# A Mamba loop issued in the order of its text, with its head pieces one per step over 18 steps and its gather three steps behind the scan

## The chip, the cores and the metric

The kernel runs on one core of one Trainium2 chip. The metric is the device time of an execution in microseconds (us); smaller is better. "Before" means the kernel before the change, "after" the changed one.

The engines are TensorE (PE, with its weight loads PEld), VectorE (DVE), ScalarE (ACT), GpSimd (POOL) and SyncE. The trace lists the instructions of each (before has 38,998 on PE, 6,112 on DVE, 5,082 on ACT and 3,186 on POOL) and says for a wait which engine's work ended it.

## The reference, cut to what matters

Four layers follow each other: a non-local block, a convolution with one Mamba, two bidirectional Mambas (along the height, then along the width), and a dynamic filter. Only the Mamba loop of layers 1 and 2 changes.

```python
def _mamba(u, p):                       # u: N sequences, L positions, 64 channels
    xz = jnp.einsum('nld,ed->nle', u, p['in_proj_w'])
    x, z = jnp.split(xz, 2, axis=-1)                        # 128 channels each
    xc = conv1d_depthwise(x, 4 taps) ; x = silu(xc + conv_b)    # written short
    dt, Bm, Cm = jnp.split(jnp.einsum('nld,ed->nle', x, p['x_proj_w']), [4, 20], axis=-1)
    dt = jax.nn.softplus(jnp.einsum('nlr,dr->nld', dt, p['dt_proj_w']) + p['dt_proj_b'])
    A = -jnp.exp(p['A_log'])                                # 128 channels x 16 states
    def step(h, inp):
        dt_t, B_t, C_t, x_t = inp
        h = jnp.exp(dt_t[:, :, None] * A) * h + dt_t[:, :, None] * B_t[:, None, :] * x_t[:, :, None]
        return (h, jnp.einsum('nds,ns->nd', h, C_t))
    _, ys = jax.lax.scan(step, h0, ...)
    y = (jnp.swapaxes(ys, 0, 1) + x * p['Dp']) * jax.nn.silu(z)
    return jnp.einsum('nld,od->nlo', y, p['out_proj_w'])
```

## The kernel before

The work is cut into 120 units of 768 positions: 24 in layer 1, 96 in layer 2, where forward and reverse units alternate. A unit has 16 steps; one step handles 16 channels with their 16 states for 384 positions, as two blocks of 128 rows by 384 columns side by side. A step n consists of:

- `spread(n+1, n+2)`: four fp32 products on PE that lay u of the next step (u_s) and dt of the step after it (dt_s) out over the states, and on ACT the exponential da of dt_s;
- `scan(n)`: on DVE the multiply u_s x B and the scan h; on POOL the product hc = h x C;
- in every second step a `gather` on PE, which sums hc over the states into y_ssm.

```python
    def spread(self, now, later):
        ...                                   # 4 products: u_s, dt_s, u_s, dt_s
        if later is not None:
            da = self.work("da", bufs=4)
            with self.k.tc.issue_after(self.table.ins):
                self.nc.scalar.activation(da, u.pda[step][...], AF.Exp)
```

Beside the steps runs the **head** of the next unit (convolution, gate, softplus, B, C), in ten pieces. Each piece is one product (`mm`, or `conv` of four taps) into the same single PSUM bank, which ACT then empties. A `yield` hands back to the loop until the next step.

```python
    def head(self, u):                        # cut
        for j in range(2):
            p = self.convolved(u, ...)
            yield
            nc.scalar.activation(u.xc[:, halves[j]], p, AF.Identity, bias=w.conv_b)
        ...                                   # two gate pieces, Silu, load of a table
        for j in range(2):
            p = self.mm(w.step, u.xc[:, halves[j]])
            yield
            nc.scalar.activation(e[:, halves[j]], p, AF.Abs, bias=w.dt_b)
            nc.scalar.activation(u.dt[:, halves[j]], p, AF.Relu, bias=w.dt_b)
        ...
        for j in range(2):
            p = self.mm(w.bc[0], u.xc[:, halves[j]])
            yield
            nc.scalar.copy(u.B[:, halves[j]], p)
        ...                                   # the same for C; log, dt, u, memset on POOL
```

Each unit of layer 1 and each reverse unit of layer 2 also has a **tail**, the output product in two halves through the same bank. The loop of before starts the next unit's head in step 1 and then the tail:

```python
        for n, (u, s) in enumerate(steps):
            if s == 1:
                other = chain(after, before)          # head of next unit, tail of last
            self.spread(at(n + 1), at(n + 2))
            self.scan(u, s)
            next(other, None)                         # one piece
            if s % 2 == 0 and n >= 2:
                self.gather(*steps[n - 1])
```

A scheduler in the compiler then decides in which order each engine gets these instructions. The `yield` between a product and its emptying says nothing about the order in the built program of before.

Of the kernel before, what the change touches and what calls it, by code (L numbers as in the profile page):

```python
# [21 lines left out]
AF = mybir.ActivationFunctionType  # L22
ALU = mybir.AluOpType
# [5 lines left out]
L = H * W  # L29
# [462 lines left out]
class Mamba:  # L492
# [10 lines left out]


    STEPS = 16

    def __init__(self, k, tables, wk, ps_da, ps_u, ps_y, ps_m):
        self.k, self.nc, self.t = k, k.nc, tables
# [30 lines left out]
    def head(self, u):  # L539
        nc, w = self.nc, u.w  # L540
        halves = [slice(j * HALF, (j + 1) * HALF) for j in range(2)]
        rows = rows_of(u.b)


        raw = self.work("raw", 2 * CH)
        u.xc, u.gate = raw[:, :CH], raw[:, CH:]
        for j in range(2):
            p = self.convolved(u, u.c0 + j * HALF)
# [3 lines that stand above are left out]
            p = self.mm(w.gate_w[rows], self.k.xb[rows, u.c0 + j * HALF : u.c0 + (j + 1) * HALF])  # L552
            yield
            nc.scalar.copy(u.gate[:, halves[j]], p)

        self.k.tc.keep_in_program_order(nc.scalar.activation(raw, raw, AF.Silu))
        self.table = nc.scalar.preload_act_table_set("natural_log_exp_and_others")
        self.k.tc.keep_in_program_order(self.table)
        yield



        e, u.dt = self.work("e", bufs=1), self.work("dt")
# [5 lines that stand above are left out]
        nc.scalar.activation(e, e, AF.Exp, scale=-1.0)  # L569
        log = self.work("log", bufs=1)  # L570
        nc.scalar.activation(log, e, AF.Ln, bias=1.0)
        u.B, u.C = self.work("B"), self.work("C")
        for j in range(2):
            p = self.mm(w.bc[0], u.xc[:, halves[j]])
            yield
            nc.scalar.copy(u.B[:, halves[j]], p)
        kept = self.work("kept", bufs=1)
        nc.vector.tensor_scalar(kept, e, 1.0, 1.0, ALU.add, ALU.subtract)
        nc.gpsimd.tensor_sub(e, e, kept)  # L579
        nc.gpsimd.tensor_add(log, log, e)  # L580
        p = self.mm(w.bc[1], u.xc[:, halves[0]])
        yield
        nc.scalar.copy(u.C[:, halves[0]], p)
        nc.gpsimd.tensor_add(u.dt, u.dt, log)  # L584
        u.u = self.work("u")
        nc.gpsimd.tensor_mul(u.u, u.dt, u.xc)
        if not u.carry:

            first = W - 1 if u.rev else 0
            nc.gpsimd.memset(u.dt.rearrange("p (n t) -> p n t", t=W)[:, :, first : first + 1], 1e30)  # L590
        p = self.mm(w.bc[1], u.xc[:, halves[1]])
        yield
        nc.scalar.copy(u.C[:, halves[1]], p)

    def groups(self, step):

# [10 lines left out]
    def spread(self, now, later):  # L607
# [21 lines left out]
        if later is not None:  # L629
            u, step = later  # L630
            da = self.work("da", bufs=4)
            with self.k.tc.issue_after(self.table.ins):
                self.nc.scalar.activation(da, u.pda[step][:, NB - HALF : NB + HALF], AF.Exp)  # L633
            u.da[step] = da

    def scan(self, u, step):
# [13 lines left out]
        else:  # L650
            way = slice(None, None, -1) if u.rev else slice(None)
            nc.vector.tensor_tensor_scan(h[:, way], da[:, way], bx[:, way], 0.0, ALU.mult, ALU.add)  # L652
        hc = self.work("hc", bufs=5)
        nc.gpsimd.tensor_mul(two(hc), two(h), each(u.C))  # L654
        u.hc[step] = hc

# [22 lines left out]
    def run(self, units):  # L679
# [2 lines left out]
            u.pu, u.pda, u.da, u.hc = {}, {}, {}, {}  # L682
        steps = [(u, s) for u in units for s in range(self.STEPS)]
        at = lambda n: steps[n] if n < len(steps) else None
        for _ in self.head(units[0]):
            pass
        self.spread(None, at(0))
        self.spread(at(0), at(1))
        other = iter(())
        for n, (u, s) in enumerate(steps):  # L690
            i = n // self.STEPS
            if s == 1:
                before = units[i - 1].tail(units[i - 1]) if i else ()
                after = self.head(units[i + 1]) if i + 1 < len(units) else ()
                other = chain(after, before)
            if s == self.STEPS - 2:
                for _ in other:
                    pass
            self.spread(at(n + 1), at(n + 2))
            self.scan(u, s)  # L700
            next(other, None)
            if s % 2 == 0 and n >= 2:
                self.gather(*steps[n - 1])
        self.gather(*steps[-1])
        for _ in units[-1].tail(units[-1]):
            pass


# [11 lines left out]
def layer1(k):  # L720
# [41 lines left out]
    with ExitStack() as pools:  # L762
# [10 lines left out]
        def tail(u):  # L773
            rows = rows_of(u.b)
            for j in range(2):
# [3 lines left out]
                out = k.xa[rows, u.c0 + j * HALF : u.c0 + (j + 1) * HALF]  # L779
                nc.vector.tensor_add(out, out, p[rows, :HALF])  # L780

        m.run(
            [
                SimpleNamespace(w=w, b=b, c0=c0, rev=False, carry=carries[b], tail=tail)
                for c0 in range(0, L, CH)
                for b in range(B)
            ]
        )


def layer2(k):
# [5 lines left out]
def bi_mamba(k, which, along_h, lin_w, lin_b):  # L797
# [27 lines left out]
    with ExitStack() as pools:  # L825
# [46 lines left out]
        for c0 in range(0, L, CH):  # L872
            for b in range(B):
                f = SimpleNamespace(w=w[0], b=b, c0=c0, rev=False, carry=None, tail=no_tail)
                r = SimpleNamespace(w=w[1], b=b, c0=c0, rev=True, carry=None, tail=tail, forward=f)
                units += [f, r]
        m.run(units)


def layer3(k, out):  # L880
# [134 lines left out]
```

## Time and profile before

| | before |
|---|---|
| time | 10,242.94 us, median of 3 (10,217.05 to 10,250.11) |
| unit, layer 1 / layer 2 along H / along W | 59.3 / 56.6 / 55.8 us |
| mean granted clock in the loop, same parts | 0.78 / 0.84 / 0.84 |
| outside the loop | about 3,410 us |

The unit times are the distances between the Silu of successive units.

Then two groups of PE, with busy time, mean ns of one, and the idle time before them with what ended most of it:

```profile
L622 PE MATMUL u_s<-u,spread 32*128 32x384 f32 x7680 | 2221.5, 629 | 429.3 <-DVE h L652 325.5
...
L513 PE MATMUL mm<-raw,bc 128*128 128x384 f32 x960 | 519.2, 627 | 27.7 <-ACT dt L568 23.0
```

The second says that the head's products almost never wait. From the view of waits, the weight loads that go ahead of such a product (us in total, times, longest). They wait more often than the products: at 7030.12 PEld has been idle for 0.55 us before such a load, ended by ACT's copy of B, and PE not at all before the product:

```profile
PEld mm L513 <- ACT B L576: 123.1, 213, 1.7
```

And a window over 47 units of layer 2 (window, length, then busy us of PE, PEld, DVE, ACT, POOL, then the clock):

```profile
4528.20:7187.00 2658.80, 2263.99 (x10676) 751.71 (x10676) 2083.68 (x1667) 1132.36 (x1544) 1771.98 (x1068) 0.84 0.00 1
```

DVE is busy for 2,084 of 2,659 us. The rest is what a better order could win.

### The profile page before, as it was taken

What the parts mean: (1) busy time and instruction counts of PE and PEld (TensorE: products, weight loads), DVE (VectorE), ACT (ScalarE), POOL (GpSimd) and SP (SyncE); (2) the same over time, 40 slices, a digit from 0 to 9 for tenths busy, and PEclk for the clock granted to TensorE, in tenths of its full rate; (3) what the DMA queues carried; (4) which work ended last, traced back from release to release, by engine and by line L of the source; (5) the groups of instructions that cost most, each with busy time, mean ns of one, the idle gap of its engine ahead of it and who ended that gap; (6) DMA issues with size and microseconds to landing.
All of it is one profiled execution on the core that took longest, in us unless ns stands there. A gap on an engine that the chain in (4) does not pass through costs nothing.

```text
span 10211.9 us, 100390 instructions
## 1 busy us (share of the span) xinstructions
PE 8743.6 (86%) x38998; PEld 2948.9 (29%) x38998; DVE 7503.5 (73%) x6112; ACT 4291.8 (42%) x5082; POOL 4701.9 (46%) x3186
## 2 busy tenths in 40 slices
PE   9999999999868888868888888888688888888884
PEld 3333333333222222222222222222222222222221
DVE  4666646666658777767787777777778777787778
ACT  3444434444334334434444444444344444444442
POOL 0000000000036666636666666666367666676663
PEclk9999989999977777768888888888688888898887
DMA  0000000000000000000000000000000000000000
GB/s 24 1 1 1 1 1 1 1 1 1 1 0 1 1 1 1 1 0 1 1 1 1 1 1 1 1 1 1 0 1 1 1 1 1 1 1 1 1 1 19
DMA packets 2220, 17.25 MB, mean 2 GB/s; under 512 B 196, under 2 KB 324, under 8 KB 1096
## 3 DMA queue, kind: packets, MB, share of 16 engines
q1 hardware_dynamic: 1440, 9.44, 0.2%
q8 instruction: 307, 5.03, 0.2%
q14 instruction: 177, 1.45, 0.0%
q10 hardware_dynamic: 296, 1.33, 0.0%
HBM read 6.05 MB, written 4.72 MB: 1 GB/s over the span
## 4 chain that ended last, share of the span: by engine, by line
PE 27%; DVE 24%; POOL 15%; issue 5%; ACT 2%; DVEq 0%; POOLq 0%; ACTq 0%
DVE h L652 13%; PE u_s L622 7%; POOL hc L654 7%; DVE u_s L642 7%; PE y_ssm L665 6%; PE conv L536 4%; PE mm L513 4%; POOL e L579 2%; POOL log L580 2%; POOL dt L584 2%; PE dt_s L622 1%; PE conv L530 1%; DVE h L648 1%; POOL yg L677 1%; PE lin L863 1%
## 5 line engine op out<-in xcount | busy, mean ns | idle before, releaser
L654 POOL TENSOR_TENSOR hc<-h,C 128x768 f32<-128x768 f32 x1920 | 3484.0, 1819 | 1746.0 <-DVE h L652 1551.5
L652 DVE TENSOR_TENSOR_SCAN h<-da,u_s 128x768 f32<-128x768 f32 x1536 | 2693.8, 1754 | 199.5 <-DVE u_s L642 4.8
L633 ACT ACTIVATE da<-dt_s 128x768 f32<-128x768 f32 x1920 | 1554.2, 809 | 2936.6 <-PE dt_s L622 2914.2
L642 DVE TENSOR_TENSOR u_s<-u_s,B 128x768 f32<-128x768 f32 x1920 | 1825.6, 951 | 1146.0 <-PE dt_s L622 1059.0
L622 PE MATMUL u_s<-u,spread 32*128 32x384 f32 x7680 | 2221.5, 629 | 429.3 <-DVE h L652 325.5
L622 PE MATMUL dt_s<-dt,decay 32*128 32x384 f32 x7680 | 2119.3, 630 | 8.7 <-ACT da L633 3.5
L267 DVE TENSOR_TENSOR acc_e<-acc_e,e 128x1536 f32<-128x1536 f32 x792 | 1390.0, 1755 | 763.4 <-ACT e L211 724.7
L665 PE MATMUL y_ssm<-hc,gather 128*32 128x384 f32 x7680 | 1433.9, 598 | 457.9 <-POOL hc L654 456.6
L211 ACT ACTIVATE e<-f_exp 128x1536 f32<-128x1536 f32 x864 | 1207.0, 1449 | 1218.4 <-PE f_exp L201 1218.4
L622 PEld LDWEIGHTS u_s<-u,spread 32*128 32x128 f32 x7680 | 775.5, 217 | 1871.8 <-DVE h L652 805.9
L240 POOL TENSOR_TENSOR xa<-xa,t_att 64x512 f32<-64x512 f32 x36 | 45.3, 1259 | 2725.1 <-ACT t_att L238 2725.1
L218 PE MATMUL y_att<-e,xb 128*64 128x512 f32 x5184 | 1242.5, 601 | 0.0
L201 PE MATMUL f_exp<-theta,phi 64*128 64x512 f32 x5184 | 1235.7, 608 | 0.6 <-ACT e L211 0.6
L536 PE MATMUL conv<-xb,taps 64*128 64x384 f32 (+3 forms) x1536 | 694.2, 604 | 118.2 <-ACT raw L550 117.5
L648 DVE TENSOR_TENSOR_SCAN h<-da,state,u_s 128x384 f32<-128x384 f32 x768 | 737.4, 1000 | 48.4 <-DVE u_s L642 1.0
L622 PEld LDWEIGHTS dt_s<-dt,decay 32*128 32x128 f32 x7680 | 692.4, 217 | 186.7 <-ACT da L633 126.7
L201 PEld LDWEIGHTS f_exp<-theta,phi 64*128 64x128 f32 x5184 | 468.8, 187 | 756.7 <-issue 463.4
L665 PEld LDWEIGHTS y_ssm<-hc,gather 128*32 128x32 f32 x7680 | 232.0, 116 | 1429.7 <-POOL hc L654 854.4
L218 PEld LDWEIGHTS y_att<-e,xb 128*64 128x64 f32 x5184 | 341.3, 136 | 830.7 <-issue 830.1
L513 PE MATMUL mm<-raw,bc 128*128 128x384 f32 x960 | 519.2, 627 | 27.7 <-ACT dt L568 23.0
L550 ACT ACTIVATE raw<-conv,cols 128x384 f32<-128x384 f32 x240 | 139.6, 582 | 909.6 <-PE conv L536 415.1
L536 PEld LDWEIGHTS conv<-xb,taps 64*128 64x128 f32 x1536 | 332.7, 227 | 457.1 <-ACT raw L550 180.4
(147 smaller groups left out, 6005.7 us busy)
## 6 DMA issues: line engine op xcount, KB each, us to landing
xa<-in_x SPq DMA_DIRECT2D x6, 768.0 KB, 10.1
out<-xb SPq DMA_DIRECT2D x4, 1152.0 KB, 4.4
mats<-in_mats ACTq DMA_DIRECT2D x1, 1218.0 KB, 7.8
cols<-in_cols ACTq DMA_DIRECT2D x1, 71.5 KB, 9.5
dtw<-in_dtw ACTq DMA_DIRECT2D x1, 10.0 KB
```

Of the source, the lines that this page charges most:

```text
L201: nc.tensor.matmul(fs[j // 3][:, bass.ts(j % 3, NB)], lhsT=phi[at, bass.ts(m // 2, P)], rhs=theta[at, bass.ts(i, NB)], start=True, stop=True,)
L211: nc.scalar.activation(e, f, AF.Exp)
L218: nc.tensor.matmul(y[rows_of(m % 2)], lhsT=g[:, m, :], rhs=es[j // 3][:, bass.ts(j % 3, NB)], start=m < 2, stop=m >= KEYS - 2,)
L267: nc.vector.tensor_add(acc, acc, e)
L513: self.nc.tensor.matmul(p[:, :HALF], lhsT=lhsT, rhs=rhs, start=True, stop=True)
L536: self.nc.tensor.matmul(p3[:, :, o], lhsT=lhsT, rhs=x3[:, :, i], **flags)
L622: self.nc.tensor.matmul(self.side((u.pu if what == 0 else u.pda)[step], j), lhsT=(self.t.spread if what == 0 else u.w.decay)[rows, q], rhs ...
L633: self.nc.scalar.activation(da, u.pda[step][:, NB - HALF : NB + HALF], AF.Exp)
L642: nc.vector.tensor_mul(two(bx), two(bx), each(u.B))
L652: nc.vector.tensor_tensor_scan(h[:, way], da[:, way], bx[:, way], 0.0, ALU.mult, ALU.add)
L654: nc.gpsimd.tensor_mul(two(hc), two(h), each(u.C))
L665: nc.tensor.matmul(u.py[32 * r : 32 * r + 32, :HALF], lhsT=self.t.gather[:, q], rhs=u.hc[s][:, j * HALF : (j + 1) * HALF], start=q == 0, s ...
```

## The change

Its intent is to take the order out of the scheduler's hands and spread the work evenly, so that DVE, the engine with the most unavoidable work (45.4 us in a unit of layer 2 against PE's 34 at full clock, by the prediction's sums), never waits: head pieces one per step over 18 steps instead of bunched, POOL's chain of four pieces pulled apart, gathers late enough never to wait for POOL.

```diff
+    LEAD = 18
...
-        raw = self.work("raw", 2 * CH)
+        raw = self.work("raw", 2 * CH, bufs=3)
...
-        for j in range(2):
-            p = self.mm(w.bc[0], u.xc[:, halves[j]])
-            yield
-            nc.scalar.copy(u.B[:, halves[j]], p)
-        kept = ...; nc.gpsimd.tensor_sub(e, e, kept)      (these three put short)
+        for t, lhsT in ((u.B, w.bc[0]), (u.C, w.bc[1])):
+            for j in range(2):
+                p = self.mm(lhsT, u.xc[:, halves[j]])
+                yield
+                nc.scalar.copy(t[:, halves[j]], p)
+                if lhsT is w.bc[0] and j == 1:
+                    kept = ...; nc.gpsimd.tensor_sub(e, e, kept)
+
         nc.gpsimd.tensor_add(log, log, e)
         yield
+        yield
         nc.gpsimd.tensor_add(u.dt, u.dt, log)
+        yield
+        yield
         u.u = self.work("u")
         nc.gpsimd.tensor_mul(u.u, u.dt, u.xc)
...
-            with self.k.tc.issue_after(self.table.ins):        (and two more such hints)
-                self.nc.scalar.activation(da, ...)
+            self.nc.scalar.activation(da, ...)
...
-        hc = self.work("hc", bufs=5)
+        hc = self.work("hc", bufs=7)
...
+            i, ahead = (n + self.LEAD) // self.STEPS, (n + 2) // self.STEPS
+            if i not in heads and 0 < i < len(units):
+                heads[i] = self.head(units[i])
...
+            if s == self.STEPS // 2 + 1 and n > s:
+                before = units[n // self.STEPS - 1]
+                tail = before.tail(before)
             self.spread(at(n + 1), at(n + 2))
             self.scan(u, s)
-            next(other, None)
-            if s % 2 == 0 and n >= 2:
-                self.gather(*steps[n - 1])
+            for one in (*heads.values(), tail):
+                next(one, None)
+            if s % 2 == 0 and n >= 4:
+                self.gather(*steps[n - 3])
...
-        m.run(units)
+        with tc.manual_schedule():
+            m.run(units)
```

With `manual_schedule` the text is the program. The head's `yield` between product and emptying now does mean that the copy is issued one step later, after the next `spread` and its da.

More of the change, by code (lines that the diff above doesn't have):

```diff
@@ L554, in head @@
             nc.scalar.copy(u.gate[:, halves[j]], p)
-        self.k.tc.keep_in_program_order(nc.scalar.activation(raw, raw, AF.Silu))
-        self.table = nc.scalar.preload_act_table_set("natural_log_exp_and_others")
-        self.k.tc.keep_in_program_order(self.table)
+        nc.scalar.activation(raw, raw, AF.Silu)
+        nc.scalar.preload_act_table_set("natural_log_exp_and_others")
         yield
@@ L572, in head @@
         u.B, u.C = self.work("B"), self.work("C")
-        for j in range(2):
-            p = self.mm(w.bc[0], u.xc[:, halves[j]])
-            yield
-            nc.scalar.copy(u.B[:, halves[j]], p)
-        kept = self.work("kept", bufs=1)
-        nc.vector.tensor_scalar(kept, e, 1.0, 1.0, ALU.add, ALU.subtract)
-        nc.gpsimd.tensor_sub(e, e, kept)
+        for t, lhsT in ((u.B, w.bc[0]), (u.C, w.bc[1])):
[4 more added lines that the diff above has]
+                if lhsT is w.bc[0] and j == 1:
+                    kept = self.work("kept", bufs=1)
+                    nc.vector.tensor_scalar(kept, e, 1.0, 1.0, ALU.add, ALU.subtract)
+                    nc.gpsimd.tensor_sub(e, e, kept)
         nc.gpsimd.tensor_add(log, log, e)
-        p = self.mm(w.bc[1], u.xc[:, halves[0]])
         yield
-        nc.scalar.copy(u.C[:, halves[0]], p)
+        yield
         nc.gpsimd.tensor_add(u.dt, u.dt, log)
+        yield
+        yield
         u.u = self.work("u")
@@ L590, in head @@
             nc.gpsimd.memset(u.dt.rearrange("p (n t) -> p n t", t=W)[:, :, first : first + 1], 1e30)
-        p = self.mm(w.bc[1], u.xc[:, halves[1]])
-        yield
-        nc.scalar.copy(u.C[:, halves[1]], p)
     def groups(self, step):
@@ L631, in spread @@
             da = self.work("da", bufs=4)
-            with self.k.tc.issue_after(self.table.ins):
-                self.nc.scalar.activation(da, u.pda[step][:, NB - HALF : NB + HALF], AF.Exp)
+            self.nc.scalar.activation(da, u.pda[step][:, NB - HALF : NB + HALF], AF.Exp)
             u.da[step] = da
@@ L684, in run @@
         at = lambda n: steps[n] if n < len(steps) else None
+        heads = {}
         for _ in self.head(units[0]):
@@ L688, in run @@
         self.spread(at(0), at(1))
-        other = iter(())
+        tail = iter(())
         for n, (u, s) in enumerate(steps):
-            i = n // self.STEPS
-            if s == 1:
-                before = units[i - 1].tail(units[i - 1]) if i else ()
-                after = self.head(units[i + 1]) if i + 1 < len(units) else ()
-                other = chain(after, before)
-            if s == self.STEPS - 2:
-                for _ in other:
-                    pass
+            i, ahead = (n + self.LEAD) // self.STEPS, (n + 2) // self.STEPS
+            if i not in heads and 0 < i < len(units):
+                heads[i] = self.head(units[i])
+            if ahead in heads and (n + 2) % self.STEPS == 0:
+                for _ in heads.pop(ahead):
+                    pass
+            if s == self.STEPS // 2 + 1 and n > s:
+                before = units[n // self.STEPS - 1]
+                tail = before.tail(before)
             self.spread(at(n + 1), at(n + 2))
             self.scan(u, s)
-            next(other, None)
-            if s % 2 == 0 and n >= 2:
-                self.gather(*steps[n - 1])
+            for one in (*heads.values(), tail):
+                next(one, None)
+            if s % 2 == 0 and n >= 4:
+                self.gather(*steps[n - 3])
+        self.gather(*steps[-3])
         self.gather(*steps[-1])
-        for _ in units[-1].tail(units[-1]):
+        for _ in chain(tail, units[-1].tail(units[-1])):
             pass
@@ L780, in tail @@
                 nc.vector.tensor_add(out, out, p[rows, :HALF])
-        m.run(
-            [
-                SimpleNamespace(w=w, b=b, c0=c0, rev=False, carry=carries[b], tail=tail)
-                for c0 in range(0, L, CH)
-                for b in range(B)
-            ]
-        )
+        units = [
+            SimpleNamespace(w=w, b=b, c0=c0, rev=False, carry=carries[b], tail=tail)
+            for c0 in range(0, L, CH)
+            for b in range(B)
+        ]
+        with tc.manual_schedule():
+            m.run(units)
 def layer2(k):
@@ L876, in bi_mamba @@
                 units += [f, r]
-        m.run(units)
+        with tc.manual_schedule():
+            m.run(units)
 def layer3(k, out):
```

## The prediction

> **What bounds the kernel now.** I read the page first: busy time per engine, the clock row, the groups. Then the timeline of two units of work, then the clock in short windows.
>
> ```profile
> PE 8743.6 (86%) x38998; PEld 2948.9 (29%) x38998; DVE 7503.5 (73%) x6112; ACT 4291.8 (42%) x5082; POOL 4701.9 (46%) x3186
> ...
> L652 DVE TENSOR_TENSOR_SCAN h<-da,u_s 128x768 f32<-128x768 f32 x1536 | 2693.8, 1754 | 199.5 <-DVE u_s L642 4.8
> ...
> L642 DVE TENSOR_TENSOR u_s<-u_s,B 128x768 f32<-128x768 f32 x1920 | 1825.6, 951 | 1146.0 <-PE dt_s L622 1059.0
> ```
>
> The Mamba loop is 120 units (24 in layer 1, 96 in layer 2) of 16 steps. A step is u_s and dt_s on PE, da on ACT, a multiply and a scan on DVE, hc on POOL; every second step a gather on PE. Windows over whole units gave 1363.5 us for 23 units of layer 1 (59.3 each) and 2662.0 and 2626.2 us for 47 units of layer 2 each (56.3 on average): 24 x 59.3 + 96 x 56.3 = 6830 us. The other 3410 us are not touched.
>
> Multiplies in an undisturbed row start 2.745 us apart (7051.72, 7054.46). 16 steps plus one kept (0.45) and two yv (0.5 each) make 45.4 us, so some 11 us of a layer-2 unit are waits of DVE. The third quoted line says for what: 1059 us for PE, before the multiply. PE itself has room: at full clock 16 spreads of 0.86, 8 gathers of 0.78, two conv halves of 2.7, eight mm of 0.85 and about 2 of tail are 34 us of 56. It waits and is then slow:
>
> ```profile
> 7030.50:7033.90 3.40, 3.07 (x16) 0.75 (x14) 3.27 (x4) 2.31 (x4) 3.30 (x2) 1.00 0.02 5
> 7033.90:7037.30 3.40, 0.00 (x0) 0.00 (x0) 3.26 (x3) 0.00 (x0) 3.34 (x2) 1.00 0.00 0
> 7037.50:7040.70 3.20, 3.12 (x13) 0.80 (x13) 0.00 (x0) 0.00 (x0) 3.14 (x5) 0.50 0.00 0
> ...
> 7057.90:7061.10 3.20, 1.46 (x11) 0.55 (x10) 3.07 (x3) 0.87 (x2) 2.69 (x3) 1.00 0.00 0
> 7061.30:7064.60 3.30, 3.30 (x7) 1.79 (x6) 1.87 (x2) 0.21 (x1) 1.99 (x2) 0.50 0.03 7
> ```
>
> Columns: window, length, then busy us of PE, weight loads, DVE, ACT, POOL, then the granted clock. A stretch with PE at 0.00 of 3.40, or 1.46 of 3.20, is followed by one at clock 0.50, in which the same spread takes 1.65 instead of 0.92. Over the loop the clock is 0.78 (layer 1) and 0.84 (layer 2).
>
> What before does right shows in its timeline:
>
> ```profile
> 7030.12 0.91 PE L513 MATMUL mm<-raw,bc 128*128 128x384 f32 x2
> ...
> 7030.27 0.81 ACT L633 ACTIVATE da<-dt_s 128x768 f32<-128x768 f32 x1 [0.69 <-PE dt_s L622]
> 7031.07 0.48 ACT L576 COPY B<-mm 128x384 f32<-128x384 f32 x1
> ...
> 7032.19 0.91 PE L513 MATMUL mm<-raw,bc 128*128 128x384 f32 x2
> 7032.36 0.81 ACT L633 ACTIVATE da<-dt_s 128x768 f32<-128x768 f32 x1 [0.81 <-PE dt_s L622]
> ...
> 7033.04 0.84 PE L665 MATMUL y_ssm<-hc,gather 128*32 128x384 f32 x4
> 7033.14 0.48 ACT L583 COPY C<-mm 128x384 f32<-128x384 f32 x1
> ```
>
> A head piece (mm) goes to PE straight after a spread, and ACT empties its bank (the only one for such pieces) in the same step, after that step's da. When the next piece comes, the bank is long free.
>
> [...]
>
> **The change part by part.** No operation is added or removed; order and buffers change.
>
> The program order of the changed kernel, as built, has in each step PE: spread, then mm(k), then (even steps) gather; ACT: da, then the emptying of mm(k-1). So mm(k) waits for a copy that stands behind a da that waits for the spread just ahead of mm(k). That is a ring, PE to ACT to PE, once per step, for the eleven steps after a unit's head begins (step 15 of one unit to step 9 of the next). Its length at full clock, from the timeline: spread start to dt_s end 0.92; to da 0.10; da to copy 0.80 (7030.27 to 7031.07); copy 0.48; to mm 0.05; mm to the next PE work 0.85 (7032.19 to 7033.04): 3.20 us, and 3.98 with a gather, against DVE's 2.745. Steps with Abs and Relu (about 1.05) in place of a copy are 0.55 longer.
>
> Other in-order waits, layer 2:
> - Step 14: dt_s of the next unit stands between the halves of u_s(15) and waits for the memset behind u<-dt,raw on POOL, issued in step 13. hc(13) starts 2.97 after its step; +1.8 +1.8 +0.2: PE resumes about 4.15 after step 14 begins and u_s(15) is there at 5.1, not 2.75.
> - conv halves of 2.7 each ride on steps 14 and 15, gate pieces on 0 and 1.
> - Step 2: Silu and two table loads hold ACT 4.05 us; DVE just bridges it. yv there waits for a late gather.
> - Tail (every second unit in layer 2, every unit in layer 1): its second half waits for DVE to empty the bank in step 10, and step 10's gather, for which DVE's yv waits, is behind it.
>
> Carried through by hand, step after step (a start is the later of DVE's 2.745 and the ring's arrival), starts of the multiplies in us after step 14:
>
> | step | 15 | 0 | 1 | 2 | 3 | 4 | 5 | 6 | 7 | 8 | 9 | 10 | 11 | next 14 |
> |---|---|---|---|---|---|---|---|---|---|---|---|---|---|---|
> | start | 5.1 | 9.5 | 14.65 | 18.8 | 23.35 | 26.1 | 29.25 | 33.8 | 37.5 | 41.5 | 44.7 | 48.7 | 51.95 | 60.2 |
>
> So 60.2 us at full clock: 45.4 of DVE and 14.8 of waits. A unit with a tail: lin's three matmuls of about 0.75 twice on the ring, DVE waiting from 51.5 to 56.3 for yv: 65.6. Mean 62.9. Layer 1 the same way with 2.92 per step (from its timeline), no memset wait, longer DVE, a short tail in each unit: 59.7.
>
> What it gains: before's run of four POOL pieces that held hc (DVE waited 3.43 us at 7040.72) is spread over steps 7 to 13, where POOL (1.8 + 1.8 in such a step, 1.8 in the next) catches up; gathers three steps back never wait for hc. Both are inside the figures above, since no such wait appears in them.
>
> Sum at full clock: layer 2 96 x (62.9 - 56.3) = +630; layer 1 +10. That compares my full clock with before's mixed one. A ring leaves PE holes of 1.5 us in most steps and over 3 in steps 14 and 3, so windows of half-busy PE are common: I take the clock as about 0.80, near layer 1's 0.78. About 28 of 63 us are PE work that stands on the ring (spread and mm or conv of eleven steps, six gathers). In a stretch at half clock such work takes twice as long; with 40% of the time at half clock, some 0.4 x 28 x 0.6 = 7 us per unit are added (0.6 because part of the holes fills first, a guess). 120 x 7 = 840, of which I count 500 to 840. Total 10243 + 640 + 500 to 840 = 11,380 to 11,720.
>
> **The rivals.**
> - *DVE becomes the bound.* This is what the change means to reach: 45.4 us and about 1.2 of half the tails, 46.6 per layer-2 unit and about 51 in layer 1, which saves 96 x 9.7 + 24 x 8 = 1120, giving 9,120. For it: the steps 4 to 10 of before that run at 2.745. Against it: the ring is longer than 2.745 in eleven of sixteen steps, whatever the clock.
> - *The ring at a steady clock.* Evenly spread PE work keeps the clock full: 10,880. For it: the ring's steps with bc pieces are as dense as steps of before that kept it. Against: the 4 us hole in step 14, just before conv.
> - *Half gained, half lost.* If a wait I put on the ring is missing in truth (a bank freed earlier, a shorter start), each of eleven steps loses only 0.3 and the time stays about 10,250.
> - *Low clock for good.* At half clock the ring is 1.65 + 0.10 + 0.80 + 0.48 + 0.05 + 1.6 = 4.7, or 6.1 with a gather, 5.4 on average; eleven of these and the rest make over 75 us per unit: 12,400.
>
> **Range and chances.** The order on each engine is known, and every term of the ring is read from the trace, so the sign is fairly sure; the clock is not. I take 11,400 us, 10,700 to 12,000. Faster by over 2%: 0.10, for a ring that isn't there; within 2%: 0.07; slower by over 2%: 0.83.
>
> **What would show it.** Right: in the changed profile DVE's idle time before the multiply grows from 1146 us to over 2000, released by PE; mm waits for ACT's copies (B, C, raw) in hundreds of cases; ACT's copy follows a da that ended just before; dt_s waits for POOL about 4 us once per layer-2 unit; units of layer 2 take 62 to 70 us, tail units about 5 more than others. Wrong: multiplies 2.75 apart while bc pieces run, or a mean clock over 0.92, which would make me wrong on the ring or on the clock; POOL as the releaser of the scan would mean that the lag I took as caught up isn't.

## More of the kernel before

The prediction shows the busy times and the stretches at half clock. What will be needed for the comparison beside that is, first, the clock row of the page: the span in 40 slices, each digit the granted clock in tenths.

```profile
PEclk9999989999977777768888888888688888898887
```

The first eleven slices lie ahead of the loop; then it comes, at 7 in layer 1 and mostly 8 in layer 2.

## The result, and the profile after

Ratios here are the mean time of one kernel's fast runs over that of the other's of the same rounds, so they are not quite the ratio of the medians that are quoted.

| | before | after |
|---|---|---|
| time, median of 4 | 10,229.99 us (10,191.12 to 10,250.11) | 12,625.9 us (12,614.82 to 12,628.78) |
| ratio | 1 | 1.2346 (1.2305 to 1.2386) |
| unit, layer 1 / 2 along H / along W | 59.3 / 56.6 / 55.8 | 73.8 / 77.8 / 77.4 |
| loop clock, same parts | 0.78 / 0.84 / 0.84 | 0.66 / 0.67 / 0.67 |

Slower, as predicted, but outside the predicted range of 10,700 to 12,000. The units account for all of it: 24 x 14.5 + 48 x 21.2 + 48 x 21.6 = 2,400 us, against 2,396 between the medians. From the page of after, the busy times and the clock row:

```profile
PE 9649.2 (77%) x38998; PEld 3175.5 (25%) x38998; DVE 7572.6 (60%) x6112; ACT 4218.6 (33%) x5082; POOL 4702.0 (37%) x3186
...
PEclk9999899996666665666666666666766666666666
```

The number of PE instructions is the same, and PE is busy for 906 us longer with them, while its share of the span falls. After the first slices the clock row is at 6 almost throughout. The groups:

```profile
L642 DVE TENSOR_TENSOR u_s<-u_s,B 128x768 f32<-128x768 f32 x1920 | 1840.8, 959 | 2957.7 <-PE dt_s L623 2953.8
L623 PE MATMUL u_s<-u,spread 32*128 32x384 f32 x7680 | 2845.7, 751 | 609.9 <-DVE h L652 476.3
...
L514 PE MATMUL mm<-raw,bc 128*128 128x384 f32 x960 | 536.6, 647 | 695.9 <-ACT B L577 312.7
```

DVE's idle time before the multiply grew from 1,146 to 2,958 us, all of it released by PE. The same spread product takes 751 ns instead of 629. The head's B and C products, which waited 28 us before, wait 696 us. The view of waits says how often:

```profile
DVE u_s L642 <- PE dt_s L623: 2953.8, 1081, 12.4
...
PEld mm L514 <- ACT dt L568: 692.0, 240, 3.0
PEld mm L514 <- ACT B L577: 557.0, 240, 2.5
...
PEld dt_s L623 <- POOL dt L594: 334.8, 96, 5.5
```

240 is every one of two pieces in 120 units: the products wait for ACT each time. The last line is the wait for the memset, once per unit of layer 2. (PEld is the weight load of a product. At 10376.89 both start together, PEld after 1.94 us of idle time and PE after 1.33, each ended by ACT's copy.)

A window over the same 47 units:

```profile
4875.80:8532.00 3656.20, 2655.51 (x10644) 847.94 (x10644) 2098.97 (x1662) 1102.38 (x1541) 1767.84 (x1066) 0.67 0.00 0
```

DVE, ACT and POOL do the same work as before to within 3%; only PE's work takes longer and everything else waits. The clock records of the trace hold two values only, 1.00 and 0.50 (414 stretches of each in after); in this window 67% of the time is at 0.50 and 33% at 1.00, which gives the 0.67.

The ring is easiest to see in the timeline where the clock is full (start, duration, engine, and in brackets the idle time before and what ended it):

```profile
10374.64 0.58 PE L623 MATMUL u_s<-u,spread 32*128 32x384 f32 x1
...
10375.66 0.81 ACT L633 ACTIVATE da<-dt_s 128x768 f32<-128x768 f32 x1 [1.92 <-PE dt_s L623]
10376.36 0.47 ACT L577 COPY C<-mm 128x384 f32<-128x384 f32 x1
...
10376.89 0.91 PE L514 MATMUL mm<-raw,bc 128*128 128x384 f32 x2 [1.33 <-ACT C L577]
10377.73 0.85 PE L665 MATMUL y_ssm<-hc,gather 128*32 128x384 f32 x8
...
10378.52 0.58 PE L623 MATMUL u_s<-u,spread 32*128 32x384 f32 x1
```

Spread on PE, then da on ACT, then the copy of the piece of the step before, then PE may put the next piece into the bank, then the gather, then the next spread: 10378.52 - 10374.64 = 3.88 us, while DVE needs 2.745. Two steps earlier the same ring runs at half clock:

```profile
10366.60 0.81 ACT L633 ACTIVATE da<-dt_s 128x768 f32<-128x768 f32 x1 [0.70 <-PE dt_s L623]
10367.30 0.47 ACT L577 COPY B<-mm 128x384 f32<-128x384 f32 x1
...
10367.83 1.65 PE L514 MATMUL mm<-raw,bc 128*128 128x384 f32 x2 [1.31 <-ACT B L577]
...
10369.41 1.51 PE L665 MATMUL y_ssm<-hc,gather 128*32 128x384 f32 x8
...
10372.52 0.97 DVE L642 TENSOR_TENSOR u_s<-u_s,B 128x768 f32<-128x768 f32 x1 [2.66 <-PE dt_s L623]
```

The product takes 1.65 instead of 0.91 and the gather 1.51 instead of 0.85, ACT's part is unchanged, and DVE has been idle for 2.66 us when the spread is there. The hole in step 14 looks like this:

```profile
10396.72 1.64 PE L623 MATMUL u_s<-u,spread 32*128 32x384 f32 x2 [1.81 <-DVE h L652]
...
10398.57 1.80 POOL L590 TENSOR_TENSOR u<-dt,raw 128x768 f32<-128x768 f32 x1
...
10400.43 0.11 POOL L594 MEMSET dt<- 128x8 f32 x1
...
10400.59 1.00 PE L623 MATMUL dt_s<-dt,decay 32*128 32x384 f32 x1 [2.23 <-POOL dt L594]
```

PE has put half of u_s(15) out, then stands until POOL has finished u<-dt,raw and the memset behind it, though only dt_s needs them; the other half of u_s(15) is behind dt_s. Last, the clock itself around this hole, in stretches of 3.3 to 3.4 us with the same columns as above:

```profile
10389.40:10392.80 3.40, 1.71 (x16) 0.47 (x16) 3.21 (x4) 0.81 (x1) 2.27 (x2) 1.00 0.00 0
10392.80:10396.10 3.30, 0.93 (x8) 0.31 (x8) 3.17 (x3) 0.81 (x1) 3.08 (x2) 1.00 0.00 0
10396.30:10399.60 3.30, 1.64 (x2) 0.49 (x2) 2.98 (x3) 0.00 (x0) 2.79 (x2) 0.50 0.00 0
10399.70:10403.00 3.30, 2.41 (x8) 1.02 (x9) 0.71 (x1) 0.67 (x1) 2.56 (x3) 0.50 0.00 0
10403.10:10406.40 3.30, 3.30 (x7) 1.80 (x6) 1.91 (x2) 0.04 (x1) 1.11 (x1) 0.50 0.00 0
10406.50:10409.80 3.30, 3.30 (x18) 0.72 (x16) 0.00 (x0) 0.00 (x0) 0.59 (x1) 0.50 0.00 0
```

PE is busy for 0.93 of 3.30 us in the second stretch, and the next is at 0.50. But in the last two PE is busy all the time and the clock is still 0.50; in this place it stays there for 47.8 us (10396.18 to 10443.97), with PE busy for 37.88 of them. That is what I had not reckoned with.

Step by step, the distance from one multiply to the next, mean over the units of layer 2 along W. The second column is the difference of successive starts in the prediction's table:

| step | predicted, full clock | after | in after, median at half clock |
|---|---|---|---|
| 14 | 5.1 | 5.71 | 5.7 |
| 15 | 4.4 | 8.25 | 8.4 |
| 0 | 5.15 | 8.24 | 8.4 |
| 1 | 4.15 | 6.10 | 6.1 |
| 2 | 4.55 | 6.34 | 6.6 |
| 3 | 2.75 | 2.76 | 2.76 |
| 4 | 3.15 | 3.06 | 3.1 |
| 5 | 4.55 | 6.35 | 6.4 |
| 6 | 3.7 | 4.11 | |
| 7 | 4.0 | 5.90 | 5.8 |
| 8 | 3.2 | 3.10 | |
| 9 | 4.0 | 3.88 (full clock in all) | |

The prediction is right to about 0.1 us in steps 8 and 9, which run at full clock, and in 3 and 4, which are at half clock in about half of the units and lose nothing by it. Steps 15, 0, 1, 2, 5 and 7, mostly at half clock, are 1.8 to 3.9 us longer than predicted, step 14 by 0.6. Left out are steps 11 to 13, close to what DVE needs (3.1, 2.75 and 2.74 us), and step 10, where a unit with a tail takes 8.05 us and another 3.27.

### The profile page after: what moved, and what is told of

Same layout as the page of the kernel before. It is cut to its first block, busy times and chain, and to the rows that moved or that the text cites. A ratio compares the mean times of both kernels' runs of the same rounds, so it can differ in the third digit from the quotient of the medians.

```text
span 12613.0 us, 100405 instructions
## 1 busy us (share of the span) xinstructions
PE 9649.2 (77%) x38998; PEld 3175.5 (25%) x38998; DVE 7572.6 (60%) x6112; ACT 4218.6 (33%) x5082; POOL 4702.0 (37%) x3186
## 3 DMA queue, kind: packets, MB, share of 16 engines
q10 hardware_dynamic: 296, 1.33, 0.0%
## 4 chain that ended last, share of the span: by engine, by line
PE 36%; DVE 9%; ACT 7%; issue 6%; POOL 4%; DVEq 0%; POOLq 0%; ACTq 0%
PE u_s L623 9%; PE conv L537 8%; PE mm L514 8%; PE y_ssm L665 5%; DVE h L652 4%; PE dt_s L623 3%; POOL hc L654 2%; DVE u_s L642 2%; ACT da L633 2%; POOL u L590 1%; PE lin L870 1%; ACT raw L551 1%; PE lin L874 1%; ACT raw L557 1%; ACT e L567 1%
## 5 line engine op out<-in xcount | busy, mean ns | idle before, releaser
L623 PE MATMUL u_s<-u,spread 32*128 32x384 f32 x7680 | 2845.7, 751 | 609.9 <-DVE h L652 476.3
L623 PE MATMUL dt_s<-dt,decay 32*128 32x384 f32 x7680 | 2595.8, 761 | 284.1 <-POOL dt L594 248.0
L623 PEld LDWEIGHTS u_s<-u,spread 32*128 32x128 f32 x7680 | 925.1, 252 | 2353.8 <-DVE h L652 988.0
L665 PE MATMUL y_ssm<-hc,gather 128*32 128x384 f32 x7680 | 1257.2, 740 | 9.7 <-POOL hc L654 9.7
L537 PE MATMUL conv<-xb,taps 64*128 64x384 f32 (+3 forms) x1536 | 1015.7, 838 | 136.3 <-ACT raw L551 135.6
L514 PE MATMUL mm<-raw,bc 128*128 128x384 f32 x960 | 536.6, 647 | 695.9 <-ACT B L577 312.7
L240 POOL TENSOR_TENSOR xa<-xa,t_att 64x512 f32<-64x512 f32 x36 | 45.4, 1260 | 2725.2 <-ACT t_att L238 2725.2
L623 PEld LDWEIGHTS dt_s<-dt,decay 32*128 32x128 f32 x7680 | 815.9, 255 | 446.9 <-POOL dt L594 334.8
L514 PE MATMUL mm<-raw,step 128*128 128x384 f32 x480 | 351.3, 830 | 390.0 <-ACT dt L568 223.8
L537 PEld LDWEIGHTS conv<-xb,taps 64*128 64x128 f32 x1536 | 468.2, 319 | 683.2 <-issue 429.5
L514 PE MATMUL mm<-xb,mats 64*128 64x384 f32 x480 | 367.4, 864 | 328.6 <-ACT raw L551 170.2
```

The costliest lines, as they stand in the source:

```text
L514: self.nc.tensor.matmul(p[:, :HALF], lhsT=lhsT, rhs=rhs, start=True, stop=True)
L537: self.nc.tensor.matmul(p3[:, :, o], lhsT=lhsT, rhs=x3[:, :, i], **flags)
L623: self.nc.tensor.matmul(self.side((u.pu if what == 0 else u.pda)[step], j), lhsT=(self.t.spread if what == 0 else u.w.decay)[rows, q], rhs ...
L665: nc.tensor.matmul(u.py[32 * r : 32 * r + 32, :HALF], lhsT=self.t.gather[:, q], rhs=u.hc[s][:, j * HALF : (j + 1) * HALF], start=q == 0, s ...
```

## The experiments

Two theories stood at first. **Ring and clock**: the ring stretches the steps, the thinner stream of PE work drops the clock, and the low clock stretches the ring; the two feed each other. **Rival**: the ring (or the memset wait, or the late gathers) costs all of it by itself, and the clock is only a symptom that costs little. A second rival about the cause asks whether the order alone does the harm or the rearranged text. The kernels of one call ran on one chip beside the kernel before (medians of 7: 10,211.49, 10,194.42 and 10,220.20 us in the three calls).

### The ring undone: each piece emptied in its own step

```diff
             p = self.convolved(u, u.c0 + j * HALF)
-            yield
             nc.scalar.activation(u.xc[:, halves[j]], p, AF.Identity, bias=w.conv_b)
+            yield
 (the same for the gate, step, B and C pieces; kept and sub one piece later)
```

> The changed kernel with one thing altered: each head piece is emptied by ACT in the step in which PE makes it, not one step later, so mm no longer waits for a copy behind this step's da. Theory (ring): steps 3 to 9 fall to about 2.75 us (3.1 and 3.9 at full clock, 6 at half clock now), the layer-2 unit from 78 to 55 to 58 us, the whole to about 10,200 us (9,900 to 10,700), and the clock of the loop rises to over 0.8 since PE's work sits in a shorter time. Rival (PE's work itself at half clock, 68 us per unit, is the bound whatever waits): over 11,600 us.

Measured: 10,853.01 us (10,851.92 to 10,869.31), ratio 1.0626 (1.0583 to 1.0669): 1,770 us less than after. Steps 3 to 9 took 2.76, 2.98, 4.01, 2.78, 3.19, 2.76 and 2.74 us, where after took 2.76 to 6.35. The ring is real, and moving the `yield`s (ten pieces per unit) removes most of it. The group of the B and C products, which waited 695.9 us in after:

```profile
L514 PE MATMUL mm<-raw,bc 128*128 128x384 f32 x960 | 454.3, 555 | 132.2 <-ACT B L580 127.1
```

A window over 47 units of layer 2:

```profile
4557.70:7524.80 2967.10, 2388.93 (x10644) 794.60 (x10644) 2072.67 (x1662) 1137.49 (x1541) 1763.85 (x1065) 0.74 0.00 1
```

DVE still waits 1,528 us before the multiplies (from the page's groups), and the clock rose only to 0.74; I had expected over 0.8, and the time came out a little above my range. Most of what is left are the steps 14, 15 and 0 (5.75, 8.24 and 5.38 us) around the memset's hole, and step 10 of the units with a tail (about 7.2 us where another unit takes 3.25).

### The clock alone: idle matmuls, the ring left in

```diff
+    def warm(self, now, n):
+        u, step = now
+        spare = u.pu[step][:, : NB - HALF]       # part of the PSUM tile that nobody reads
+        for _ in range(n):
+            self.nc.tensor.matmul(spare, lhsT=self.t.spread[:, 0], rhs=self.t.spread[:, 1], start=True, stop=True)
 ...                                              # in spread(), when it makes the next unit's first dt_s:
+                    self.warm(now, 14)
 ...                                              # after every spread:
+            self.warm(now, 4)
```

> The changed kernel with its ring and order intact, plus idle matmuls (4 of 128x128x128 after each spread, 14 before dt_s in step 14) into columns of the u_s tile that nobody reads. Theory (the prediction's ring was right at full clock, the low clock made the rest): clock in the loop over 0.9 instead of 0.66, steps 8 and 9 stay near 3.1 and 3.9, layer-2 unit 62 to 66 us, whole 10,800 to 11,300 us although PE does more. Rival (clock is a mere symptom; the waits set the time): 12,600 us or more.

Measured: 11,101.88 us (11,101.05 to 11,103.52), ratio 1.087 (1.0826 to 1.0914), as expected. A window over 47 units of layer 2:

```profile
4647.20:7674.70 3027.50, 2722.13 (x17852) 1468.54 (x17852) 2100.82 (x1662) 1103.28 (x1541) 1772.97 (x1065) 0.99 0.00 1
```

7,208 matmul instructions were added and the same units take 3,027.5 us instead of 3,656.2, because the clock is 0.99. Adding useless work to the engine that everyone waits for took 1,524 us off the kernel. The rival that the clock is only a symptom is out.

It also measures the predicted table at full clock: steps 14, 15, 0, 1, 2 took 6.4, 5.46, 5.06, 3.95, 4.44 us and steps 3 to 9 took 2.76, 3.01, 4.42, 3.64, 3.85, 3.07, 3.85. Apart from 14 and 15, which hold the 14 idle matmuls or start behind them, all lie within 0.2 us of the prediction; the four idle matmuls of a step (1.16 us at 8001.74 of this run, from the start of the first to the end of the last) fit into the time that PE waits for ACT on the ring (1.33 us at 10376.89 above).

### The gather ahead of the head piece

```diff
             self.scan(u, s)
-            for one in (*heads.values(), tail):
-                next(one, None)
             if s % 2 == 0 and n >= 4:
                 self.gather(*steps[n - 3])
+            for one in (*heads.values(), tail):
+                next(one, None)
```

> The changed kernel with the gather put between spread and mm, where PE waits for ACT anyway. Theory (ring): the gather leaves the ring, so an even step costs what an odd one does: 1.4 us less at half clock, 0.8 at full, in some six steps per unit, 5 to 8 us of 78: whole 11,700 to 12,000 us. Rival (PE's amount of work sets the time): within 1% of 12,626 us.

Measured: 11,993.68 us (11,993.07 to 11,999.75), ratio 1.1745 (1.1698 to 1.1793), 632 us less than after, at the upper end of what I expected. PE now does the gather while it would have waited for ACT. The steps changed in the expected places: 1 from 6.1 to 4.55, 5 from 6.35 to 5.1, 7 from 5.9 to 3.75, 9 from 3.88 to 3.10. But step 6 rose from 4.11 to 5.11, at half clock, and the loop's clock did not rise (0.65 in layer 2): a shorter ring does not by itself bring the clock back.

### POOL's pieces two steps earlier

```diff
         yield
-        yield
         nc.gpsimd.tensor_add(u.dt, u.dt, log)
         yield
-        yield
         u.u = self.work("u")
```

> The changed kernel with two empty pieces taken out, so that POOL's last three pieces of a head come in steps 9, 10 and 11 and the memset is done before step 14 needs it. Theory: step 14 of layer 2 falls from 5.7 to 2.75 us; 96 times 3 us is 285 us, so about 12,340 us; if the hole is also what sends the clock down before conv, steps 15 and 0 (8.4 each) get shorter too and it is 11,700 to 12,200 us. Rival (the wait is hidden by another that ends as late): within 1% of 12,626 us. Layer 1, which has no memset, unchanged near 75 us per unit.

Measured: 12,015.22 us (12,008.66 to 12,031.27), ratio 1.1769 (1.172 to 1.1817), 611 us less than after. The memset is done before step 14 needs it: after's wait of dt_s for POOL's dt (334.8 us) is not among the 57 largest of this run's view of waits, which go down to 52.8 us. That step falls from 5.71 to 2.74 us, step 15 from 8.25 to 5.96, step 0 from 8.24 to 6.96. Layer 1, which has no memset, stayed at 73.7 us per unit: it was this wait and not another.

### The order alone: the kernel before, in the order of its text

```diff
-        m.run(units)
+        with tc.manual_schedule():
+            m.run(units)
 (in both layers; the three ordering hints, which such a region does not allow, removed)
```

> The kernel before, its text unchanged but for its Mamba loops issued in the order of the text (the three hints that pin the table loads, which are not allowed in such a region, are gone). Theory (the order of the text makes the ring, since its pieces too are made in one step and emptied in the next behind da): as slow as the changed kernel or slower, as its gather waits one step behind the scan for POOL too: 12,600 to 13,500 us. Rival (the rearranged pieces and gathers are what costs): within 3% of before, 10,000 to 10,500 us.

Measured: 11,848.85 us (11,832.34 and 11,865.37), ratio 1.1626 (1.1558 to 1.1694), with a loop clock of 0.71 to 0.73. This is below the figure that my theory gave and far above the rival's. So the order alone costs 16%, with before's text; after's rearranged text in the order of the text takes 12,626 / 11,849, or 6.6% more than that.

### The text alone: the kernel after, handed back to the scheduler

```diff
-        with tc.manual_schedule():
-            m.run(units)
+        m.run(units)
 (and the three ordering hints of before put back)
```

> The changed kernel's text (pieces over 18 steps, gather three behind, buffers), issued by the scheduler as before, with before's three hints. Theory (the order alone costs): near before, 9,900 to 10,600 us. Rival (the rearranged text costs): over 11,500 us.

Measured: 10,245.62 us (10,228.03 and 10,263.22), ratio 1.0053 (0.9993 to 1.0113): the same as before. The 18-step lead, the larger buffers and the later gathers cost nothing and win nothing by themselves. All of the loss needs the order of the text. The loop's clock, however, is 0.73 to 0.77 here, lower than before's 0.78 to 0.84, so part of the low clock comes with the text and not with the order.

### All the known waits repaired in the hand order

```diff
 (the edits of the ring undone and of POOL's pieces earlier, together)
 and in both tails:
                 nc.vector.tensor_add(out, out, p[rows, :HALF])
+                yield
```

The last `yield` puts the tail's second half one step later, so that it does not wait for DVE to empty the bank.

> The changed kernel with every wait that I named on the ring taken away at once: pieces emptied in their own step, POOL's pieces in steps 9 to 11, the tail's second half one step later than DVE empties the first. Theory: at full clock only conv is still longer than DVE's step, so layer-2 units of 47 to 53 us depending on the clock, 9,200 to 10,000 us in all, faster than before. Rival (the clock stays at 0.5 for half the time as in the run with the pieces emptied early, because PE has holes in steps 10 to 14 in any case): 10,200 to 10,600 us.

Measured: 10,207.09 us (10,165.72 to 10,221.27), ratio 1.0004 (0.9954 to 1.0054). My theory expected 9,200 to 10,000 and missed; the rival, that the clock stays low even without these waits, held. A window over 47 units of layer 2, and the group of the multiplies:

```profile
4538.20:7167.10 2628.90, 2223.66 (x10644) 752.79 (x10644) 2066.30 (x1662) 1136.34 (x1542) 1759.90 (x1065) 0.78 0.00 1
...
L640 DVE TENSOR_TENSOR u_s<-u_s,B 128x768 f32<-128x768 f32 x1920 | 1825.9, 951 | 1145.0 <-PE dt_s L621 1140.8
```

DVE is idle before the multiplies for as long as in before (1,145 against 1,146 us in the page's groups), at a lower clock (0.78 against 0.84). Where both clocks occur one sees what each step would be: step 15 has a median of 7.57 us at half clock and 2.85 at full, step 0 6.93 and 3.59, step 5 4.62 and 2.74.

### The same with idle matmuls

```diff
+        if now is not None and now[1] in (12, 13, 14):
+            u, step = now
+            for _ in range(3):
+                self.nc.tensor.matmul(u.pu[step][:, : NB - HALF], lhsT=..., rhs=..., start=True, stop=True)
```

These are steps 11 to 13, where PE has no head piece, just before the convolution.

> The same with three idle matmuls after the spreads of steps 11, 12 and 13, which have no piece. Theory (steps without pieces let the clock fall just ahead of conv): the clock rises over that of the run without them and steps 15 and 0 lose what half clock adds there, 300 to 700 us less in all, 8,900 to 9,400 us. Rival (their 0.8 us delays the multiply): slower than the run without them.

Measured: 9,729.73 us (9,720.39 to 9,748.58), ratio 0.9549 (0.9505 to 0.9592), with a loop clock of 0.85 to 0.87. The direction and the gain of some 480 us were as expected; the time is above the range I gave, since the clock did not recover everywhere: step 5 is still at half clock in 69% of the units.

### More idle matmuls: the best version

Two versions put them into more steps: the first three of them after the spreads of steps 2, 3 and 10 to 13, the second four after those of steps 2 to 4 and 10 to 13.

```diff
-        if now is not None and now[1] in (12, 13, 14):
+        if now is not None and now[1] in (3, 4, 5, 11, 12, 13, 14):      # first: (3, 4, 11, 12, 13, 14)
-            for _ in range(3):
+            for _ in range(4):                                           # first: 3
```

> The repaired kernel (pieces emptied in their own step, POOL early, tail apart) with three idle matmuls also after the spreads of steps 2, 3 and 10, so in every step without a matmul piece. Theory (the clock falls in steps without pieces): step 5 of layer 2, at half clock in 69% of the cases before this and then 4.4 instead of 2.75 us, falls to about 3, steps 15 and 0 a little; the layer-2 unit from about 52.4 to 49 to 51, whole 9,400 to 9,650 us, clock over 0.90. Rival (step 5 is slow for the wait behind Silu, not for the clock): 9,680 to 9,780 us.

> The same with four in place of three, and after the spread of step 4 too. Theory: the clock is held in nearly all units, 9,250 to 9,600 us. Rival (1.1 us of idle matmuls per step stands in the way of mm and gather, as a step then needs 0.86 + 1.1 + 0.85 + half of 0.78 = 3.2 us of PE in step 4): equal to or slower than the run with three.

Measured: the first 9,495.62 us (9,470.96 to 9,555.93), ratio 0.9284 (0.9262 to 0.9305); the second 9,408.99 us (9,392.54 to 9,424.66), ratio 0.921 (0.9187 to 0.9232). The second beats both kernels:

```profile
L646 DVE TENSOR_TENSOR u_s<-u_s,B 128x768 f32<-128x768 f32 x1920 | 1819.5, 948 | 248.5 <-PE dt_s L621 213.0
```

```profile
4373.60:6698.90 2325.30, 2089.34 (x13224) 943.21 (x13228) 2063.16 (x1661) 1135.51 (x1541) 1764.71 (x1065) 0.97 0.00 1
```

DVE's idle time before the multiply is 249 us, and DVE is busy for 2,063 of 2,325 us. This is the DVE-bound loop that the change was meant to reach.

### The control: idle matmuls in the kernel before

```diff
+        if now is not None and now[1] in (14, 15, 0, 1, 2):
+            ...                                     # three idle matmuls, as above
```

> The kernel before, left to its scheduler, with three idle matmuls after the spreads of steps 13 to 1, the stretch without pieces ahead of its conv. Theory (before loses to the clock in the same way): its steps 3 and 11 shorten, 9,750 to 10,000 us. Rival (its waits in steps 3 and 11 are of its POOL pieces and its conv, not of the clock): within 1% of before, about 10,200 us. It also says what the order by hand is worth once the clock is held in both.

Measured: 9,756.30 us (9,754.27 to 9,758.35), ratio 0.9547 (0.953 to 0.9565), clock 0.90 to 0.94. So before, too, lost some 460 us to the clock. With the clock held up in both, though not to quite the same level, the repaired hand order is worth 9,756 to 9,409, or 3.6%; most of the best version's gain came with the clock.

### The clock beside the work of a unit: an estimate

These are counts over the records, and not a view of the profile. A product of 384 columns in fp32 is two instructions of about 0.32 us each at full clock (an estimate: conv's instructions start 0.32 us apart there in before's trace, and 0.63 at half clock). By the shapes on the page many of them have a smaller weight block than the largest, 128*128: a spread has 32*128, a gather 128*32, conv and gate 64 rows. Weighting each instruction by the size of its block against 128*128 (a choice of mine, which no run tests), a unit is worth 16 x 0.64 (spreads) + 8 x 0.64 (gathers) + 2 x 1.28 (conv) + 2 x 0.32 (gate) + 6 x 0.64 (step, B, C) + 0.8 (half a tail) = 23.2 us. An idle matmul has 128 columns and so counts for 0.214 us; the run with the ring left in has 78 of them per unit.

| layer 2 | weighted work per unit, us (estimate) | unit, us | share (estimate) | clock |
|---|---|---|---|---|
| before | 23.2 | 56.2 | 0.41 | 0.84 |
| after | 23.2 | 77.6 | 0.30 | 0.67 |
| ring undone | 23.2 | 62.6 | 0.37 | 0.74 |
| all waits repaired | 23.2 | 56.0 | 0.41 | 0.78 |
| ring left in, idle matmuls | 39.9 | 64.0 | 0.62 | 0.99 |
| best version | 29.2 | 49.1 | 0.60 | 0.97 |

The clock goes roughly with the share, not strictly: 0.41 stands beside 0.84 and beside 0.78.

Busy time alone says less. In after's 47 units above (4875.80 to 8532.00) PE was busy for 80% of the time at half clock and for 58% of the time at full clock; in before's (4528.20 to 7187.00) for 96% and 80%.

No run was made to test the weighting, with narrow idle matmuls for instance. That narrow matmuls count for less is therefore my estimate, and at what amount of work the clock falls or comes back is not shown. That added matmuls raise the clock is measured five times: in layer 2 from 0.67 to 0.99 in after, from 0.78 to 0.85 and 0.87, to 0.93 and 0.95 and to 0.97 and 0.98 in the repaired order, and from 0.84 to 0.92 and 0.94 in before.

## Why the prediction was right or wrong

**The ring was right, in place and in size.** The copies follow a da that has just ended, the products wait for them every time, and at full clock the ring takes 3.10 us, or 3.88 with a gather, against 3.20 and 3.98 predicted. Undoing it took off 1,770 us.

**The other waits were right.** dt_s waits for POOL 96 times, once per layer-2 unit, by 3.5 us on average (334.8 / 96) where I said about 4 (the parts that I added up for where PE resumes, 2.97 + 1.8 + 1.8 + 0.2 less a step of 2.745, give 4.03 and not 4.15, which changes little). A tail unit is 5.2 us longer than another along W, where I said 5.4, but 8.0 along H, which I had not told apart. POOL did not become the releaser of the scan (two waits, 1.0 us in all). The late gathers no longer wait for hc: the idle time before y_ssm fell from 457.9 to 9.7 us in the page's groups.

**The sum at full clock was right.** I said 62.9 us per layer-2 unit and +640 us. With the clock held at 0.99 the units take 64.4 and 63.7, of which steps 14 and 15, with their idle matmuls, are 2.4 us over the predicted 9.5; without those some 61.6 remain, and in layer 1 60.5 (64.0 less the 3.5 of its step 14). As an estimate, the 890 us of that run over before, less 96 x 2.4 + 24 x 3.5 = 314, leave 576.

**The step that failed is the clock's term:** "I take the clock as about 0.80", and "with 40% of the time at half clock, some 0.4 x 28 x 0.6 = 7 us per unit are added (0.6 because part of the holes fills first, a guess)", of which I counted 500 to 840 us. The runs show about 1,800 in its place: 2,396 - 576, an estimate, with 12,626 - 11,102 = 1,524 measured directly as a lower figure, since the idle matmuls cost time themselves. Both factors were too small (the 28 us were a little large; the prediction's own parts add up to some 26):

- The clock was 0.67 in layer 2, so it was half for two thirds of the time, not 40%; weighted with the prediction's full-clock durations, 72% of PE's work on the ring ran at half clock. I had read the fall of the clock off busy time, about half of PE busy (1.46 of 3.20 us in before, then 0.50), and in after 0.93 of 3.30 us is followed by 0.50 too. How the clock comes back I had not worked out; 0.80 was taken over from layer 1's 0.78. At half clock the same work is busy for twice as long (0.63 instead of 0.32 us from one of conv's instructions to the next), but that alone does not bring the clock back: in this trace a stretch with PE busy for 3.30 of 3.30 us is followed by another at 0.50. What brings it back is not shown.
- The 0.6 for "the holes fill first" came out at about 0.85, as an estimate: the units grew by 77.6 - 61.6 = 16 us, and 72% of 26 us of PE work on the ring is 19 us. A ring has next to no slack: what a product loses to the clock, the next step mostly starts later. What was hidden lies in steps such as 3 and 4, which lost nothing at half clock.

So the two feed each other, as far as the runs show: with the ring undone the clock of layer 2 rose from 0.67 to 0.74, and with the clock held at 0.99 its units, ring and all, fell from 77.6 to 64.0 us on average. It fits that undoing the ring (1,773 us) and holding the clock up (1,524 us) each won most of the loss, and together more than the 2,396 there were to win. But the ring is not the only thing that lowers the clock: with all waits repaired it was still 0.78. My rival "low clock for good", at 12,400, was nearest in number and had the right term, and I gave it too little weight. Its size is partly luck: it put all eleven steps of the ring at half clock, at 5.4 us on average, while in after a third of the time is at full clock and steps 15 and 0 take 8.2. Layer 1's units show the same at 73.8 instead of the predicted 59.7 plus the 4 to 7 us of the clock.

**What the change was meant to win** exists: 9,409 us is not far above the 9,120 of the first rival. It needs the copies in their own step, POOL's pieces earlier, and above all the clock. Repairing the waits alone gives 10,207, no more than before. What stays open is why the repaired order runs at a lower clock than before (0.78 against 0.84) with the same work per unit. The text of after in the scheduler's order has a low clock too (0.75 and 0.77 in layer 2), so the spacing of the pieces is suspect rather than the order by hand. I suspect that the even spread leaves too little PE work in stretches such as steps 11 to 13, as the gain of the idle matmuls placed there fits (0.78 to 0.85 and 0.87), but no run isolates it.

## What to carry to other kernels

When instructions go out in the order of the text, look for a ring: a piece that needs a bank, whose emptying is queued behind something that needs the piece's own engine. Empty it in the step that fills it, and compare the ring's length with the bound engine's step. Do not price a thinner stream of TensorE work by its busy share alone (in after PE was busy for 80% of the time at half clock and for 58% of the time at full), count nearly all of the loss where the work is on a ring, and when the granted clock is well below 1 on a path that waits for TensorE (0.84 here), try a few idle matmuls before rearranging anything: in the kernel before they won 4.5% in a few lines. A second bank for the pieces was not tried here.
